# Exchanging the queues of the first loads and reordering the first and last batch of a cross-attention kernel

## The chip, the core and the metric

The kernel runs on one core of one Trainium2 chip. The metric is the device time of one execution in microseconds (us); lower is better. Three timed runs of the kernel before the change gave 660.87, 660.82 and 661.15 us, median 660.87. One more execution was profiled; every view below is of that one.

## The reference

For each of 8 batches, `x1` (512 x 1024) gives queries and `x2` (512 x 1024) gives keys and values; the attention is taken over the 1024 positions and `x1` is added to the result.

```python
q = einsum('bcn,dc->bnd', x1, Wq) + bq                # d = 64
k = einsum('bcn,dc->bdn', x2, Wk) + bk[:, None]
v = einsum('bcn,dc->bdn', x2, Wv) + bv[:, None]       # 512 channels
attn = softmax(einsum('bnd,bdm->bnm', q, k), axis=2)  # 1024 x 1024
out = einsum('bcm,bnm->bcn', v, attn) + x1
```

## The kernel before

All data are float32, and the large products are split: an operand becomes a high part `h`, a low part `l` and a sum part `d` in the format fp32r, and one product is three matmul passes. ScalarE (ACT) rounds the high parts and copies out of PSUM, VectorE (DVE) makes the low and sum parts, GpSimd (POOL) reduces over partitions and issues accumulating DMAs, SyncE (SP) issues plain DMAs. Only the first two value units and output units of batch 0 go in plain float32 (`VF`, `RF`), two slower passes for each product, without a split.

The order of all work is written out by hand, in lists of words, and each word is a call of a method of `Batch`. `FIRST` is for batch 0, `MIDDLE` for batches 1 to 6, `LAST` for batch 7; a word with `+` belongs to the next batch, one with `-` to the previous one. Every engine executes its own instructions in the order of the words; between engines semaphores hold an instruction until its data and its buffer are there. The words that matter here:

- `hx.c`, `hw.c` (called by `begin()`): the loads of quarter `c` of the channels of the first chunk of x2 (128 KB each) and of the value weights (256 KB each). `ldx2.0`, `ldx2.1`: the second chunk (512 KB), and the third and fourth together (1 MB). `lwq`: the weights of q and k, and their bias. `lsd`: the bias of v. `ldx1.0`, `ldx1.1`: x1, in halves.
- `wh.z wl.z wd.z w4.z`: the split of the value weights, on ACT and DVE in turn. `xh.k xl.k xd.k`: the split of chunk k of x2 (256 positions, two value units).
- `K`, `Q`: the projections on TensorE (PE); they use all chunks of x2, or all of x1. `ke`, `qe` take them out of PSUM (ACT), `kc`, `qd` copy them to the other half of the partitions (SP's DMAs), `kr kl`, `qr ql` split them.
- value unit j (128 positions): `VX.j` makes two passes into a bank X, `VY.j` one pass into a bank Y that `sy.j` has filled with the bias (ACT); `cy.j` copies Y out (ACT), `jn.j` joins both (DVE). `vh vl vd` split a pair of units.
- `S.h.i`: scores; `Sc.h.i` copies them out (ACT); `F.Q T.Q L.u E.u` maximum, subtraction and exponential; `es a1 a2 a3 tot few rec r2` the sums; `H.u l.u d.u` split the exponentials of unit u; `R.u.m` is the product with the values; `oy o oa st` take it out, add x1 and store it.

Banks and tiles go round: X and Y have 3 banks each, the scores and projections (`sc`) 2, and x1 and x2 share 2 buffers. `begin()` also runs 10 small matmuls on zeros (`ps_warm`) ahead of the first real one. In the head of the program SP has the four `hx` and ACT the four `hw`:

```python
for c in range(CT):
    states[0].hx(c)      # nc.sync.dma_start(... x2[0, :, 0, c])
    states[0].hw(c)      # nc.scalar.dma_start(... wvT[c])
```

Of the kernel before, what the change touches and what calls it, by code (L numbers as in the profile page):

```python
# [35 lines left out]
vd.2 S.1.5 S.1.3 Sc.1.3 T.0 L.0 E.0 F.1 S.1.6 S.1.4 Sc.1.4 Sc.1.5 L.1 E.1 es.0 VX.6 jn.6 RF.0.0 T.1 L.2 L.3
S.1.7 a1.0 Sc.1.6 RF.0.1 RF.0.2 RF.0.3 RF.0.4 Sc.1.7 F.2 RF.0.5 +ldx2.0 +qd +qr +ql sy.7 VY.7 cy.7 jn.7 vh.3
T.2 L.4 E.2 H.2 a2.0 a3.0 +ldx2.1 +K +ke +kc RF.1.0 L.5 vl.3 vd.3 tot.0 few.0 RF.1.1 RF.1.2 RF.0.6 RF.0.7 l.2
d.2 E.3 H.3 es.1 l.3 a1.1 d.3 E.5 RF.1.3 RF.1.4 E.4 H.4 es.2 rec.0 r2.0 of.0 oa.0 st.0 RF.1.5 RF.1.6 RF.1.7
R.2.0 R.2.1 R.2.2 H.5 R.2.3 F.3 R.2.4 R.2.5 R.2.6 R.2.7 R.3.0 R.3.1 a2.1 a3.1 +kr +kl +S.0.0 +S.0.1 +Sc.0.0  # L40
+Sc.0.1 R.3.2 of.1 R.3.3 l.4 T.3 L.7 E.7 H.7 d.4 +S.0.2 +Sc.0.2 R.3.4 R.3.5 R.3.6 l.5 l.7 +S.0.3 +Sc.0.3 a1.2
a2.2 a3.2 L.6 +S.0.4 +Sc.0.4 R.3.7 +S.0.5 +Sc.0.5 R.4.0 R.4.1 +S.0.6 tot.1 few.1 rec.1 d.5 d.7 oa.1 st.1 tot.2
few.2 +S.0.7 R.4.2 R.4.3 R.4.4 R.4.5 R.4.6 R.4.7 r2.1 oy.2 oy.3 o.2 o.3 oa.2 oa.3 st.3 +Sc.0.6 +Sc.0.7 +F.0
E.6 H.6 es.3 l.6 a1.3 d.6 rec.2 r2.2 oy.4 st.2 +T.0 +L.0 +L.1 +E.0 +E.1 +es.0 +F.1 o.4 oa.4 st.4 a2.3 a3.3
R.5.0 R.5.1 R.5.2 R.5.3 R.5.4 R.5.5 R.5.6 R.5.7 oy.5 o.5 oa.5 st.5 +xh.0 +xl.0 +xh.2 +xl.2 +xd.0 +xh.1 +xl.1
# [37 lines left out]
def kernel(  # L83
# [45 lines left out]
    def bank(tag, name):  # L129
        return psum.tile([P, H], F32, tag=tag, name=name, bufs=BUFS[tag])  # L130

    class Batch:
# [30 lines left out]
        def hx(self, c):  # L163
            if c == 0:
                self.x2[0] = new([P, 2, CT, QN], "x", "x2_0_0")
            nc.sync.dma_start(self.x2[0][:, 0, c, :], x2[0, :, 0, c])

        def hw(self, c):
            if c % 2 == 0:
                wraw[c // 2] = new([P, 2, C], "kd", f"w_raw{c // 2}")  # L170
            nc.scalar.dma_start(wraw[c // 2][:, c % 2, :], wvT[c])

        def lwq(self):
            nc.sync.dma_start(wqk_sb, wqk)
            nc.sync.dma_start(bqk_sb, bqk)
# [339 lines left out]
    def begin():  # L515
        for c in range(CT):
            states[0].hx(c)
            states[0].hw(c)
# [1 line left out]
        nc.vector.memset(spark, 0.0)  # L520

        for i, times in enumerate((4, 3, 3)):
            ps = bank("Y", f"ps_warm{i}")
            for k in range(times):
                nc.tensor.matmul(
                    ps, warm, warm.unsqueeze(1).to_broadcast([P, 4, P]), start=(k == 0), stop=(k == times - 1)
                )
# [48 lines left out]
```

## Time and profile before

| what | value |
|---|---|
| median of 3 timed runs | 660.87 us (660.82 to 661.15) |
| the profiled execution's own time | 661.69 us |
| its span on the core | 659.9 us |
| PE busy | 652.8 us, 99% |
| DVE busy | 619.0 us, 94% |
| ACT busy | 452.4 us, 69% |
| POOL busy | 203.5 us, 31% |
| DMA, mean over the span | 137 GB/s |
| granted TensorE clock, by slices | 9 tenths or more in all 40 |

The own time of the profiled execution is 1.8 us longer than its span: that much lies before the first and behind the last instruction. Engines run side by side, so the shares do not add. PE is busy nearly all the time; a busy PE row does not say that its passes run at their best rate. What can change the time is where PE has nothing to do: at the beginning, at the end and where it waits.

### The profile page before, as it was taken

To read this page: it belongs to the slowest core of one execution; us is meant where nothing else is said; L and a number is where in the kernel's file an instruction comes from. 1 tells how busy PE (TensorE), PEld (TensorE's weight loads), DVE (VectorE), ACT (ScalarE), POOL (GpSimd) and SP (SyncE) were. 2 spreads that over 40 slices of the span, in tenths; PEclk is the share of its full clock that TensorE was granted. 3 is DMA by queue.
4 is the path that set the end of the run, shared out by engine and by line. 5 is a ranking of instruction groups with operands and counts; after the bars stand their busy time and mean duration, and the time that the engine had idled before them with its cause. 6 is when DMAs were issued, how large, how long until landed. Compare 5 with 4: busy or idle time off the path is not lost.

```text
span 659.9 us, 8059 instructions
## 1 busy us (share of the span) xinstructions
PE 652.8 (99%) x2802; PEld 492.4 (75%) x2802; DVE 619.0 (94%) x689; ACT 452.4 (69%) x670; POOL 203.5 (31%) x162
## 2 busy tenths in 40 slices
PE   8999999999999999999999999999999999999997
PEld 3664888677886688866888668886688776887886
DVE  4789999999999999999999999999999999999994
ACT  5688676876587675876767757677675975759542
POOL 0014432323414333043520335212352214412451
PEclk9999999999999999999999999999999999999999
DMA  8534648364665647474563745737367275632374
GB/s 316 191 96 107 119 98 221 73 201 96 129 175 112 175 98 163 124 173 120 114 173 96 216 100 111 173 83 224 81 128 179 77 207 98 126 81 49 93 150 124
DMA packets 41464, 90.21 MB, mean 137 GB/s; under 512 B 13136, under 2 KB 13904, under 8 KB 37712
## 3 DMA queue, kind: packets, MB, share of 16 engines
q0 software_dynamic: 13536, 33.04, 30.0%
q1 hardware_dynamic: 27312, 55.62, 25.4%
q10 hardware_dynamic: 576, 1.05, 0.4%
q8 instruction: 22, 0.36, 0.2%
q14 instruction: 18, 0.15, 0.1%
HBM read 51.91 MB, written 16.78 MB: 104 GB/s over the span
## 4 chain that ended last, share of the span: by engine, by line
PE 96%; DMA 2%; ACT 1%; DVEq 0%; issue 0%; ACTq 0%; DVE 0%
PE ps_oX L426 34%; PE ps_oY L426 17%; PE ps_vX L386 17%; PE ps_s L262 9%; PE ps_vY L386 8%; PE ps_k L205 4%; PE ps_q L205 4%; PE ps_o L451 2%; DMA x<-in_x_dram 1%; DMA w_raw<-in_wvT_dram 1%; ACT eh L297 0%; ACT e L293 0%; ACT ps_vY L382 0%; ACT vy L401 0%; ACT es L312 0%; ACT vh L408 0%
## 5 line engine op out<-in xcount | busy, mean ns | idle before, releaser
L426 PE MATMUL ps_oY<-vd,ed 128*128 128x512 f32 x496 | 193.2, 392 | 0.0
L426 PE MATMUL ps_oX<-vh,eh 128*128 128x512 f32 x496 | 193.0, 389 | 0.0
L426 PE MATMUL ps_oX<-vl,el 128*128 128x512 f32 x496 | 193.0, 389 | 0.0
L426 PEld LDWEIGHTS ps_oY<-vd,ed 128*128 128x128 f32 x496 | 93.1, 188 | 25.0 <-issue 5.1
L506 POOL DMA_DIRECT2D o<-in_x1T_dram x62 | 55.6, 916 | 171.6 <-ACT o L503 97.6
L426 PEld LDWEIGHTS ps_oX<-vl,el 128*128 128x128 f32 x496 | 93.1, 188 | 19.5
L426 PEld LDWEIGHTS ps_oX<-vh,eh 128*128 128x128 f32 x496 | 93.1, 188 | 19.3 <-issue 0.2
L293 ACT ACTIVATE e<-e 128x1024 f32<-128x1024 f32 x64 | 67.9, 1062 | 49.6 <-DVE e L290 48.3
L267 ACT COPY e<-ps_s 128x512 f32<-128x512 f32 x128 | 70.9, 589 | 28.6 <-PE ps_s L262 27.6
L329 POOL PARTITION_ALL_REDUCE den<-es x32 | 80.7, 2522 | 26.0 <-DVE es L319 25.0
L306 DVE SCALAR_TENSOR_TENSOR ed<-el,eh 128x1024 fp32r<-128x1024 f32 x62 | 83.0, 1341 | 2.1
L315 POOL DMA_DIRECT2D es<-e x32 | 28.6, 895 | 179.1 <-ACT es L312 166.9
L301 DVE TENSOR_TENSOR el<-e,eh 128x1024 fp32r<-128x1024 f32 x62 | 79.5, 1298 | 0.0
L290 DVE TENSOR_TENSOR e<-e,top 128x1024 f32<-128x1024 f32 x64 | 77.0, 1231 | 0.0
L282 POOL PARTITION_ALL_REDUCE top<-max x32 | 46.9, 1466 | 68.0 <-DVE max L278 67.9
L386 PE MATMUL ps_vX<-wh,xh 128*128 128x512 f32 x248 | 67.6, 394 | 0.0
L386 PE MATMUL ps_vY<-wd,xd 128*128 128x512 f32 x248 | 65.9, 393 | 0.8 <-ACT ps_vY L382 0.8
L386 PE MATMUL ps_vX<-wl,xl 128*128 128x512 f32 x248 | 66.3, 389 | 0.0
L297 ACT ACTIVATE eh<-e 128x1024 fp32r<-128x1024 f32 x62 | 64.6, 1054 | 0.5
L401 ACT COPY vy<-ps_vY 128x512 f32<-128x512 f32 x62 | 36.4, 591 | 40.0 <-PE ps_vY L386 38.8
L386 PEld LDWEIGHTS ps_vX<-wh,xh 128*128 128x128 f32 x248 | 45.8, 188 | 15.7 <-DVE max L277 4.1
L386 PEld LDWEIGHTS ps_vY<-wd,xd 128*128 128x128 f32 x248 | 46.2, 188 | 12.5 <-ACT ps_vY L382 1.6
(59 smaller groups left out, 963.5 us busy)
## 6 DMA issues: line engine op xcount, KB each, us to landing
x<-in_x_dram SPq DMA_DIRECT2D x29, 1024.0 KB, 6.6
es<-e POOLq DMA_DIRECT2D x32, 512.0 KB, 4.6
out_dram<-o SPq DMA_DIRECT2D x63, 256.0 KB, 2.4
o<-in_x1T_dram POOLq DMA_DIRECT2D x62, 256.0 KB, 4.3
x<-in_x_dram SPq DMA_DIRECT2D x5, 512.0 KB, 10.3
k<-k SPq DMA_DIRECT2D x16, 128.0 KB, 2.2
q<-q SPq DMA_DIRECT2D x16, 128.0 KB, 2.4
w_raw<-in_wvT_dram ACTq DMA_DIRECT2D x4, 256.0 KB, 4.1
```

The costliest lines, as they stand in the source:

```text
L205: nc.tensor.matmul(ps[r, :], wqk_sb[:, which, c, :], x(h, c), start=(c == 0), stop=(c == CT - 1))
L262: nc.tensor.matmul(ps, k[:, ts(i, P)], self.qa[:, ts(h, H)], start=(z == 0), stop=(z == 1))
L267: nc.scalar.copy(self.half[h][:, :, i, :], self.ps[h, i].rearrange("p (q n) -> p q n", q=2))
L290: nc.vector.tensor_tensor(e, e, top, ALU.subtract)
L293: nc.scalar.activation(self.unit(u), self.unit(u), AF.Exp)
L297: nc.scalar.activation(self.e[u]["h"], self.unit(u), AF.Copy, scale=SPLIT)
L301: nc.vector.tensor_tensor(self.e[u]["l"], self.unit(u), f32(self.e[u]["h"]), ALU.subtract)
L306: nc.vector.scalar_tensor_tensor(e["d"], f32(e["l"]), -T, f32(e["h"]), ALU.mult, ALU.add)
L329: nc.gpsimd.partition_all_reduce(self.den[Q], self.es[Q][:, 0, :], P, ReduceOp.add)
L386: nc.tensor.matmul(ps, self.c[j // 2][z][:, c, ts(j % 2, P)], w[z][:, c, :], start=(start and c == 0), stop=(stop and c == CT - 1), skip_g ...
L426: nc.tensor.matmul(ps, self.e[u][z][:, m, :], self.v[m // 2][z][:, m % 2, :], start=start, stop=stop, skip_group_check=True,)
L506: nc.gpsimd.dma_start(self.o[u], x1T[self.b, ts(u, P), :], accum_op=ALU.add)
```

## The change

The same 336 words of `FIRST` and 235 words of `LAST` stand in another order; no word is added or removed, and `MIDDLE` is untouched. In the head, `hx` goes to ACT's queue and `hw` to SP's, the load of the bias of q and k moves from SP (`lwq`) to the end of ACT's head loads, and one of the ten warming matmuls is left out. On PE the float32 passes of units 0 and 1 now go quarter by quarter (`VF.0.c VF.1.c`), and behind `K` come `VY.3`, `VX.2`, `Q`, `VX.3`, `VY.2`, `VY.4`, `VX.5`, `VY.5`, `VX.4` and then the first scores. The methods `xh`, `xl`, `xd` can leave out half of a chunk (`apart`), but with `WHOLE = 2` the test `k == 0.5` is never true, and they do what they did.

In a few words the change was described as: head's loads exchanged between the queues, first passes of value unit 2 ahead of k's projection, order of first and last batch anew with delays in mind. In the list itself `K` stands ahead of `VX.2`, as before.

```diff
-VF.0.0 VF.1.0 VF.1.1 wh.0 VF.1.2 VF.1.3 wl.0 wd.0 w4.0 wh.1 wl.1 wd.1 w4.1 VF.0.1 VF.0.2 VF.0.3 lwq ldx2.0
-ldx2.1 xh.1 lsd K xl.1 xh.2 xh.3 ldx1.0 bv ke xd.1 xl.2 xl.3 VX.2 ldx1.1 jf.0 xd.2 xd.3 sy.2 sy.3 sy.5 jf.1 Q
-kc VY.2 VY.3 qe kr cy.2 cy.3 vh.0 qd kl jn.2 vl.0 qr sy.4 VX.3 jn.3 vh.1 VX.4 VY.5 cy.5 vd.0 VX.5 VY.4 cy.4 ql
-S.0.0 S.0.1 S.0.2 S.0.3 S.0.5 Sc.0.0 Sc.0.1 Sc.0.2 Sc.0.3 S.0.4 Sc.0.4 Sc.0.5 S.0.6 Sc.0.6 S.0.7 Sc.0.7 S.1.1
...
+wh.0 VF.0.0 VF.1.0 wl.0 VF.0.1 VF.1.1 wd.0 wh.1 VF.0.2 VF.1.2 wl.1 VF.0.3 VF.1.3 wd.1 w4.1 ldx2.0 lwq xh.1
+xl.1 xd.1 w4.0 ldx2.1 lsd K xh.3 bv xl.3 jf.0 xd.3 sy.2 sy.3 sy.4 jf.1 VY.3 cy.3 ldx1.0 ke VX.2 xh.2 xl.2 xd.2
+vh.0 vl.0 vd.0 ldx1.1 Q kc qe kr VX.3 kl VY.2 cy.2 jn.2 jn.3 sy.5 +ldx1.0 qd qr VY.4 cy.4 VX.5 vh.1 VY.5 cy.5
+VX.4 ql S.0.0 S.0.1 S.0.2 S.0.3 S.0.7 Sc.0.0 Sc.0.1 Sc.0.2 Sc.0.3 S.0.4 Sc.0.4 jn.4 jn.5 vh.2 vl.1 vd.1 vl.2
...
 LAST = """
...
-vh.0 vl.0 d.1 E.3 es.1 sy.3 VY.3 H.0 l.0 cy.2 jn.2 sy.4 VY.4 cy.3 jn.3 d.0 a3.0 Sc.1.2 a1.1 vd.0 sy.5 vh.1
-vl.1 a2.1 S.1.4 vd.1 S.1.3 Sc.1.3 Sc.1.4 tot.0 few.0 cy.4 jn.4 -r2.3 -os.6 -oa.6 -st.6 VY.5 cy.5 VX.5 jn.5
+vh.0 vl.0 d.1 E.3 es.1 sy.3 VY.3 H.0 l.0 cy.2 jn.2 sy.4 VY.4 cy.3 jn.3 a3.0 Sc.1.2 a1.1 vd.0 sy.5 vh.1 vl.1
+a2.1 vd.1 S.1.3 Sc.1.3 tot.0 few.0 cy.4 jn.4 S.1.4 Sc.1.4 d.0 -r2.3 -os.6 -oa.6 -st.6 VY.5 cy.5 VX.5 jn.5 VX.6
...
-... H.3 r2.0 T.2 L.4 L.5 E.4 E.5 es.2 d.2 R.2.0 ... lt a1.2 H.5 d.3 ...
+... H.3 r2.0 T.2 L.5 L.4 E.5 H.5 E.4 es.2 d.2 R.2.0 ... lt a1.2 d.3 ...
-... rec.3 r2.3 oy.6 oy.7 t.6 t.7 o.6 o.7 st.6 st.7 p.7 sq.7
+... rec.3 r2.3 oy.6 oy.7 t.6 o.6 st.6 t.7 o.7 st.7 p.7 sq.7
...
+    WHOLE = 2
...
         def hx(self, c):
...
-            nc.sync.dma_start(self.x2[0][:, 0, c, :], x2[0, :, 0, c])
+            nc.scalar.dma_start(self.x2[0][:, 0, c, :], x2[0, :, 0, c])
         def hw(self, c):
...
-            nc.scalar.dma_start(wraw[c // 2][:, c % 2, :], wvT[c])
+            nc.sync.dma_start(wraw[c // 2][:, c % 2, :], wvT[c])
         def lwq(self):
             nc.sync.dma_start(wqk_sb, wqk)
-            nc.sync.dma_start(bqk_sb, bqk)
...
+        def apart(self, k):
+            return slice(P, QN) if self.first and k == WHOLE / 2 - 0.5 else slice(0, QN)
...
             states[0].hw(c)
+        nc.scalar.dma_start(bqk_sb, bqk)
...
-        for i, times in enumerate((4, 3, 3)):
+        for i, times in enumerate((3, 3, 3)):
```

More of the change, by code (lines that the diff above doesn't have):

```diff
@@ L36 @@
[L36 to L45, printed above, removed]
@@ new lines @@
+VX.4 ql S.0.0 S.0.1 S.0.2 S.0.3 S.0.7 Sc.0.0 Sc.0.1 Sc.0.2 Sc.0.3 S.0.4 Sc.0.4 jn.4 jn.5 vh.2 vl.1 vd.1 vl.2
+S.0.6 S.0.5 Sc.0.5 Sc.0.6 Sc.0.7 F.0 T.0 L.0 L.1 F.1 S.1.1 sy.6 +ldx1.1 +Q +qe S.1.0 Sc.1.0 Sc.1.1 S.1.7 vd.2
+VX.6 S.1.2 Sc.1.2 E.0 VY.6 cy.6 jn.6 S.1.4 T.1 L.2 L.3 S.1.3 Sc.1.3 Sc.1.4 VX.7 S.1.6 +ldx2.0 E.1 es.0 S.1.5
+Sc.1.5 Sc.1.6 Sc.1.7 F.2 RF.0.0 RF.0.1 RF.0.2 RF.0.3 RF.0.4 a1.0 +qd +qr +ql RF.0.5 E.2 H.2 l.2 E.3 H.3 es.1
+a2.0 a3.0 +ldx2.1 +K +ke +kc RF.1.0 RF.1.1 RF.1.2 sy.7 VY.7 cy.7 RF.1.3 RF.1.4 RF.1.5 T.2 L.4 L.5 E.4 H.4 +kr
@@ new lines @@
+jn.7 vh.3 RF.0.6 RF.1.6 RF.0.7 a1.1 d.2 F.3 tot.0 few.0 rec.0 r2.0 of.0 oa.0 st.0 a2.1 E.5 H.5 es.2 l.3 a3.1
+RF.1.7 R.2.0 R.2.1 R.2.2 R.2.3 R.2.4 R.2.5 of.1 +kl +S.0.0 +S.0.1 +Sc.0.0 +Sc.0.1 d.3 R.3.0 R.3.1 R.3.2 +S.0.2
++Sc.0.2 R.3.3 +S.0.3 +Sc.0.3 +S.0.4 +Sc.0.4 R.3.4 R.3.5 vl.3 T.3 L.6 L.7 E.7 +S.0.5 +Sc.0.5 H.7 vd.3 R.2.6
+R.3.6 R.2.7 R.3.7 l.4 d.4 R.4.0 a1.2 a2.2 +S.0.6 +Sc.0.6 l.5 R.4.1 tot.1 few.1 rec.1 r2.1 oy.3 a3.2 d.5 +S.0.7
+l.7 d.7 oa.1 st.1 oy.2 o.2 tot.2 few.2 R.4.2 R.4.3 R.4.4 R.4.5 R.4.6 R.4.7 oa.2 st.2 o.3 oa.3 st.3 +Sc.0.7
@@ L48 @@
++F.0 E.6 H.6 es.3 l.6 a1.3 d.6 +xh.0 rec.2 r2.2 oy.4 +T.0 +L.0 +L.1 +E.0 +E.1 +es.0 +xh.1 o.4 oa.4 st.4 +xl.0
++xd.0 +F.1 R.5.0 R.5.1 R.5.2 R.5.3 R.5.4 R.5.5 R.5.6 R.5.7 oy.5 o.5 oa.5 st.5 a2.3 +xl.1 a3.3 +xd.1 +xh.3
++xl.3 R.6.0 R.6.1 R.6.2 R.6.3 R.6.4 R.6.5 R.6.6 R.6.7 oy.6 o.6 R.7.0 R.7.1 R.7.2 R.7.3 +sy.0 R.7.4 R.7.5 R.7.6
+R.7.7 oy.7 o.7 +xh.2 +xl.2 +xd.2 +sy.1 +S.1.0 +Sc.1.0 +S.1.1 +Sc.1.1 tot.3 few.3 rec.3
 """
@@ L348, in chunk @@
             return self.x2[k // 2][:, k % 2]
+        def apart(self, k):
+            return slice(P, QN) if self.first and k == WHOLE / 2 - 0.5 else slice(0, QN)
         def xh(self, k):
+            at = self.apart(k)
             self.c[k] = {"h": new([P, CT, QN], "kh", f"xh_{self.b}_{k}", FR)}
-            nc.scalar.activation(self.c[k]["h"], self.chunk(k), AF.Copy, scale=-SPLIT)
+            nc.scalar.activation(self.c[k]["h"][:, :, at], self.chunk(k)[:, :, at], AF.Copy, scale=-SPLIT)
         def xl(self, k):
-            self.c[k]["l"] = new([P, CT, QN], "kl", f"xl_{self.b}_{k}", FR)
-            nc.vector.tensor_tensor(self.c[k]["l"], self.chunk(k), f32(self.c[k]["h"]), ALU.add)
+            c, at = self.c[k], self.apart(k)
+            c["l"] = new([P, CT, QN], "kl", f"xl_{self.b}_{k}", FR)
+            nc.vector.tensor_tensor(c["l"][:, :, at], self.chunk(k)[:, :, at], f32(c["h"][:, :, at]), ALU.add)
         def xd(self, k):
-            c = self.c[k]
+            c, at = self.c[k], self.apart(k)
             c["d"] = new([P, CT, QN], "kd", f"xd_{self.b}_{k}", FR)
-            nc.vector.scalar_tensor_tensor(c["d"], f32(c["l"]), T, f32(c["h"]), ALU.mult, ALU.add)
+            nc.vector.scalar_tensor_tensor(
+                c["d"][:, :, at], f32(c["l"][:, :, at]), T, f32(c["h"][:, :, at]), ALU.mult, ALU.add
+            )
         def VF(self, j, c):
```

15 lines of the change are left out of this document (6 added, 9 removed).

## The prediction

> **What bounds the kernel now.** I read the page's busy shares first, then PE's waits, then the chain of waits, then the head's timeline.
>
> ```profile
> PE 652.8 (99%) x2802; PEld 492.4 (75%) x2802; DVE 619.0 (94%) x689; ACT 452.4 (69%) x670; POOL 203.5 (31%) x162
> PE ps_k L205 <- DMA x<-in_x_dram: 1.4, 1, 1.4
> PE ps_warm L525 <- DVE spark L520: 1.0, 1, 1.0
> PE ps_vY L386 <- ACT ps_vY L382: 0.8, 1, 0.8
> PE ps_s L262 <- ACT e L267: 0.2, 1, 0.2
> 14.51 3.65 PE ps_k L205 x14
> 18.16 2.04 PE ps_vX L386 x8
> 20.20 3.58 PE ps_q L205 x16
> ...
> 590.30 0.92 PE ps_vY L386 x4
> 591.25 0.59 ACT vy L401
> ```
>
> PE has four waits in the whole execution. One is the start, one is in the head (K waits for a load), and two are in the last batch. In the chain PE stands alone from 14.51 to 591: each piece begins where the one before it ended. A new order of the same words can therefore gain nothing in that stretch; it can only bring new waits. What can be gained lies ahead of 14.51, in the 1.0 us of waits in batch 7, and behind the last matmul.
>
> **The head, as it is.**
>
> ```profile
> 0.73 4.17 ACTq L171 DMA_DIRECT2D w_raw<-in_wvT_dram  x4
> 0.73 1.80 SPq L166 DMA_DIRECT2D x<-in_x_dram  x4
> 2.58 0.43 SPq L174 DMA_DIRECT2D wqk_sb<-in_wqk_dram  x1
> 4.32 0.33 SPq L175 DMA_DIRECT2D bqk_sb<-in_bqk_dram  x1
> 4.56 0.34 ACTq L171 DMA_DIRECT2D w_raw<-in_wvT_dram  x1
> 5.12 0.80 SPq L161 DMA_DIRECT2D x<-in_x_dram  x2
> 8.39 0.30 PEld L366 LDWEIGHTS ps_v<-w_raw,x 128*128 128x128 f32 x2 [0.77 <-DMA w_raw<-in_wvT_dram]
> 12.02 0.19 PEld L205 LDWEIGHTS ps_k<-x,wqk_sb 128*64 128x64 f32 x2 [0.76 <-DMA x<-in_x_dram]
> 14.51 0.20 PEld L205 LDWEIGHTS ps_k<-x,wqk_sb 128*64 128x64 f32 x4 [2.30 <-DMA x<-in_x_dram]
> GB/s 0 0 42 190 300 356 382 391 395 354 284 360 257 333 410 391 404 431 399 429 421 421 421 197 87 33 49 208 98 0 0 0 0 0 167 199 191 279 355 448
> ```
>
> Eight loads are issued by 3 us; the ninth and tenth (bias, fourth weight quarter) go out only at 4.32 and 4.56, as the first ones land. So the fourth quarter of wv comes late, and PE's float32 passes stop for about 0.5 us until 8.39. Then K begins at 12.02, when the second chunk of x2 is there, and stops until 14.51 for chunks 3 and 4 (`ldx2.1`, 1 MB). The last row is the bandwidth in slices of 0.75 us from 0 to 30: it is at 380 to 430 GB/s except for a ramp (42, 190, 300) and a weak stretch from 6.75 to 10.5 (354, 284, 360, 257, 333).
>
> **The change, part by part.**
>
> *Exchange of the queues, bias to ACT, quarters in step.* SP now has the four weight loads, so the fourth goes out near 2.1 instead of 4.56, and `VF.0.3 VF.1.3` come last. 16 passes at 0.43 (successive rows 8.92 and 9.35 of the same line below) are 6.9 us; from a start near 4.6 they end near 11.5 instead of 11.9. The 0.5 us stop goes. What is late next is K: its second pair of matmuls still needs chunks 3 and 4, and K stands ahead of every other PE work that is ready. So the stop moves into the wait for `ldx2.1`, and only the landing of that load counts, one for one. The wait of the ninth and tenth load stays: it now falls on the bias (ACT) and chunk 2 (SP, near 4.5 instead of 5.12). Behind the bias on ACT wait the table load and `wh.0`, as they did behind the fourth weight load until 4.9; their result is first used behind K. Behind chunk 2 on SP wait wqk and `ldx2.1`.
>
> When does `ldx2.1` land? Ahead of it in the same bandwidth lie, before and after, the same bytes: 4 x 128 KB, 4 x 256 KB, 256 KB for wqk, 512 KB and its own 1 MB. Only lost bandwidth can be won. Best end: the weak stretch fills up to 395: (41 + 111 + 35 + 138 + 62) x 0.75 us = 290 KB, at 390 GB/s 0.74 us, and the queue that starts first carries rows of double size in the first slice (42 x 0.75 = 32 KB, 0.1 us): 0.85 us earlier. Worst end: `ldx2.1` has to wait one 256 KB load longer for its turn, 0.66 us later. Before, that stretch was not short of issued loads (5.12 and 5.6 lie well ahead of it), and reissuing them sooner gives it nothing; the row it is nearest to is the same load's own landing at 14.5. I take 0.2 us earlier: the ramp's 0.1 and a small part of the weak stretch. [...]
>
> *One warming matmul less.*
>
> ```profile
> 3.94 0.15 PEld L525 LDWEIGHTS <-warm 128*128 128x128 bf16 x1 [0.28 <-issue]
> 4.37 0.14 PEld L525 LDWEIGHTS <-warm 128*128 128x128 bf16 x1 [0.28 <-issue]
> 4.63 0.41 PEld L366 LDWEIGHTS ps_v<-w_raw,x 128*128 128x128 f32 x2
> 8.92 0.19 PEld L366 LDWEIGHTS ps_v<-w_raw,x 128*128 128x128 f32 x1 [0.24 <-issue]
> 9.35 0.19 PEld L366 LDWEIGHTS ps_v<-w_raw,x 128*128 128x128 f32 x1 [0.24 <-issue]
> ```
>
> 0.26 us at most (4.37 to 4.63), and hidden by the wait for `ldx2.1`: nothing. If that cover went, the first passes would still wait for the first weights near 4.5, so 0.1.
>
> *The order behind K.* PE's work from K to the first scores is the same: before VX.2, Q, VY.2, VY.3 and so on, after VY.3, VX.2, Q, then VX.3, VY.2, VY.4, VX.5, VY.5, VX.4. VY.3 needs the bank filled by `sy.3`, behind `xh.3`, `bv` and `sy.2` on ACT: 14.3, 1.06 for a rounding (the row of `qr` below) and three times 0.59 (the copy of 128x512 above) make 17.1, ahead of K's end near 18. `cy.3` now stands ahead of `ke` on ACT and holds it for VY.3's 0.9 us and its own 0.6, with k's copies behind it; k is next used after q, so nobody waits. The tight place is q.
>
> ```profile
> 23.83 1.40 ACT L212 ACTIVATE q<-ps_q,bqk_sb 64x512 f32<-64x512 f32 x2 [2.59 <-PE ps_q L205]
> 29.78 1.06 ACT L235 ACTIVATE qa<-q 128x1024 fp32r<-128x1024 f32 x1 [1.41 <-DMA q<-q]
> 31.39 1.22 DVE L238 TENSOR_TENSOR qa<-q,qa 64x1024 fp32r<-64x1024 f32 x1
> 32.69 0.19 PEld L262 LDWEIGHTS ps_s<-qa,kh 128*128 128x128 f32 x1
> q<-q SPq DMA_DIRECT2D x1, 128.0 KB, 2.2
> q<-q SPq DMA_DIRECT2D x1, 128.0 KB, 4.4
> x<-in_x_dram SPq DMA_DIRECT2D x29, 1024.0 KB, 6.6
> ```
>
> Before, q's second copy was issued when `qe` was done (23.83 + 1.40 = 25.2) and landed 4.4 us later; its rounding began at once (29.78), and the scores began in the moment that `ql` was done (31.39 + 1.22 = 32.61 to 32.69). After: K from 14.3 to 17.95, VY.3 0.92 (the chain's row of four passes), VX.2 twice that, 1.84, and 0.1 for changing over, so Q from 20.8 to 24.4, 0.6 us later than before, and `qe` done at 25.8; the copy, then `qr` and `ql`, 1.06 and 1.22. The scores' turn on PE is at 24.4 + 3 x 1.84 + 3 x 0.92 = 32.7. With a copy of 2.2 us q is ready at 30.3, with 4.4 us at 32.5: only just. Ahead of `qd` on SP now stands batch 1's first x1 load (1 MB), which stood behind it. It needs only k's copies issued ahead of it and the first x2 buffer, free when K ends, and `ke` ends near 21 (17.95 + 0.92 + 0.6 + 1.4), so it has some 4 us of lead, and its bytes (1 MB at 400 GB/s, 2.6 us) are mostly through when the copies come. I put in 0.1 us, between 0 and the 2.0 of the second rival.
>
> *The rest of FIRST.* The same words, with no PE wait before, so 0 at best. In the list, the producers that PE waits for (`Sc` for reused banks, `d` for `R`, `jn` for reused X banks) still stand several words ahead of their users. I take 0, with 0.5 us at the other end (half of batch 7's 1.0, where the order is as tight).
>
> *LAST.*
>
> ```profile
> 601.14 1.22 DVE L306 SCALAR_TENSOR_TENSOR ed<-el,eh 128x1024 fp32r<-128x1024 f32 x1
> 607.53 1.28 DVE L404 SCALAR_TENSOR_TENSOR v<-ps_vX,vy 128x512 f32<-128x512 f32 x2
> 608.26 1.21 PE L386 MATMUL ps_vX<-wh,xh 128*128 128x512 f32 x4
> 618.68 3.25 DVE L290 TENSOR_TENSOR e<-e,top 128x1024 f32<-128x1024 f32 x2
> 621.86 1.21 DVE L306 SCALAR_TENSOR_TENSOR ed<-el,eh 128x1024 fp32r<-128x1024 f32 x1
> 623.13 0.50 PE L426 MATMUL ps_oY<-vd,ed 128*128 128x512 f32 x1
> 656.25 0.48 DVE L491 SCALAR_TENSOR_TENSOR o<-ps_oX,r,oy 128x256 f32<-128x256 f32 x1 [1.55 <-PE ps_oX L426]
> ```
>
> The 0.8 us wait of VY.4 is for `sy.4` on ACT (L382 in the list of waits), and ACT's order up to it is unchanged: it stays. `S.1.4` and `S.1.3` change places, but the third score of the group still needs the copy out of the first: the 0.2 us stays. `d.0` (1.22 at 601.14) moves behind `jn.4`, which comes forward from 607.53 and frees the bank of VX.7 a little sooner (0.68 each for the two joins: 608.2, against VX.7's 608.26). That is given back at 623.13: R.2.0 begins when `d.2` is done (621.86 + 1.21), at the end of DVE's unbroken work, whose sum is the same. `H.5` ahead of `E.4` and `es.2` delays `es.2` by 1.06 us; its next user, `a1.2`, comes much later. At the end `o.6` and its store come sooner, but the last pieces wait for PE's last matmul (656.25). Sum 0, between -0.3 and +0.3.
>
> **The sum.** -0.2 + 0.1 + 0 = -0.1 us. On the profiled execution's own time that is 661.69 to 661.6; the median of the runs lies 0.8 below that execution, so 660.87 becomes 660.8.
>
> **The rivals.**
>
> *The stream ahead of K gets much denser.* If the exchange repairs the ramp too (lost against 390: (348 + 200 + 90 + 34) x 0.75 = 504 KB, 1.3 us) along with the weak stretch (0.74), `ldx2.1` lands up to 2 us earlier; three quarters of it are 1.5 us: 659.4. For it: the wait for K is one for one. Against it: the ramp is the same number of loads from the same two queues. 0.12.
>
> *q's copy is held behind the 1 MB load now ahead of it on SP* (slower). Place: `qr`, then `ql`, then all scores. If the copy takes 6.6 us, as a 1 MB load does, q is ready at 34.7 and S.0.0 begins 2.0 us late: 662.8. It decides from a landing more than 4.6 us after issue. Against it: the load has 4 us of lead. 0.07.
>
> *PE's clock falls back in the longer pause.* The warming rows are 0.43 apart while PE starts and 0.26 at the last: PE began at half its rate. PE would pause from 11.5 to 14.3, broken by one pair of K near 12. Half rate for K adds its 3.6 us once more: 664.4. Against it: after the pause that ends at 14.51 now, K took 3.65, no longer than Q's 3.58 without a pause. 0.03. [...]
>
> *The change does what its description says, not its list:* value unit 2 ahead of K fills 0.9 us of the pause (four passes; the other four need `w4.0`, which stands behind `xh.1` on ACT and ends near 14): 659.9. The list has K first. 0.02.
>
> **How the numbers follow.** The forecast has 0.76: 660.8, by its bounds (-0.85 to +0.66, q up to 0.5, the rest 0.3) 660.0 to 661.9. With half of the first rival, the range is 659.6 to 662.0. A measurement of this kernel tells about 0.2%, 1.3 us, from no change. Faster than 659.5: the first rival and a tail, 0.13. Slower than 662.2: q's copy, the clock and unseen waits in FIRST, 0.10. Within: 0.77.
>
> **What would show it.** Right: K's second pair waits for x until 14.0 to 14.6; no wait in the float32 passes; PE unbroken from K to batch 7; VY.4's 0.8 us wait still there. Wrong: K going on before 13.5, a wait of ps_s for qa near 32.7, K longer than 4 us from its last load, or a wait of PE for DVE between 40 and 120.

## The result, and the profile after

The changed kernel is slower: 663.27 us median of five runs (663.06 to 664.76) beside 660.87 for the kernel before; the ratio is 1.0043 with a 95% interval of [1.0032, 1.0054]. The prediction was 660.8 in a range of 659.6 to 662.0. The profiled execution of the changed kernel took 663.27 us, its span is 661.5.

From the page after: the busy shares, and the chain that ended last by engine.

```profile
PE 654.5 (99%) x2801; PEld 493.0 (75%) x2801; DVE 619.4 (94%) x689; ACT 452.7 (68%) x670; POOL 202.6 (31%) x162
PE 90%; DVE 6%; ACT 1%; issue 1%; DMA 1%; POOL 0%; DVEq 0%; SPq 0%; POOLq 0%
```

PE's waits after, without the one at the start (total, times, longest, in us):

```profile
PE ps_vY L395 <- ACT ps_vY L391: 1.0, 2, 0.8
PE ps_s L263 <- ACT e L268: 0.8, 3, 0.4
PE ps_oY L435 <- DVE ed L307: 0.3, 1, 0.3
PE ps_oY L435 <- DVE r L339: 0.2, 1, 0.2
```

K's wait for its load (1.4 before) is gone from the list, and new waits for ACT and DVE are there. Where they are, the chain after shows (start, length):

```profile
12.79 4.38 PE ps_k L206 x16
...
91.73 2.25 DVE e L291 x2
102.45 2.64 POOL den L330
105.64 4.90 DMA few<-den
111.42 2.27 DVE e L291 x2
...
147.66 3.58 PE ps_k L206 x16
548.95 3.58 PE ps_k L206 x16
```

The chain before was PE alone from 14.51 to 591. Ahead of batch 7, this one leaves PE between 91 and 121 and runs through DVE, a total on POOL (`tot.3`), its small loads (`few.3`) and DVE again. The last two rows are K as it stands in the words of batches 1 and 6 (each makes the k of the next batch). In the chain of the kernel before the same two are:

```profile
146.76 3.58 PE ps_k L205 x16
547.51 3.58 PE ps_k L205 x16
```

Five middle batches, whose words nobody touched, take 401.29 us after and 400.75 before, without a single wait of PE in either: 0.11 us more per batch. Two losses, then: one between 90 and 121, one spread evenly over the batches behind it.

For the runs below I use one number of the trace that the head hardly disturbs: the time from the first pass of R.2.0 (at 66.56 before, 65.58 after) to the end of the span. It is 593.36 us before and 595.92 after, 2.56 more: 1.88 up to the first of these rows, 0.54 between the two, 0.14 behind. It comes from one profiled execution of each kernel; in six kernels that should agree in it (before, new head, new LAST, and below all tiles moved by 64 and `vd.3` by 512 and 1024) it lies between 593.29 and 593.52, so a difference under 0.2 tells nothing. The head itself varies from execution to execution: in the nine profiles of this study with the old head the first value pass behind K begins between 16.33 and 18.64, in the eleven with the new head between 16.37 and 19.91 (medians 17.55 and 16.98). The profile of before in the prediction was a late one (18.09).

Each ratio is against runs of the kernel before on the same chip (medians 660.65 to 660.87).

| kernel | median us | ratio to before [95%] | R.2.0 to end |
|---|---|---|---|
| before | 660.87 | 1 | 593.36 |
| after | 663.27 | 1.0043 [1.0032, 1.0054] | 595.92 |
| new head alone | 660.68 | 0.9997 [0.9988, 1.0006] | 593.29 |
| new LAST alone | 660.97 | 1.0005 [0.9997, 1.0014] | 593.36 |
| before, vd.3 displaced | 661.81 | 1.0017 [1.0009, 1.0026] | 594.03 |
| after, vd.3 as before | 662.7 | 1.0032 [1.0020, 1.0044] | 595.54 |
| new order up to F.2 | 660.98 | 1.0007 [0.9997, 1.0017] | 593.81 |
| new order behind F.2 | 663.24 | 1.0031 [1.0020, 1.0043] | 595.14 |

### The profile page after: what moved, and what is told of

The parts are those of the page before. It is cut to its first block, busy times and chain, and to the rows that moved or that the text cites. A ratio compares the mean times of both kernels' runs of the same rounds, so it can differ in the third digit from the quotient of the medians.

```text
span 661.5 us, 8060 instructions
## 1 busy us (share of the span) xinstructions
PE 654.5 (99%) x2801; PEld 493.0 (75%) x2801; DVE 619.4 (94%) x689; ACT 452.7 (68%) x670; POOL 202.6 (31%) x162
## 4 chain that ended last, share of the span: by engine, by line
PE 90%; DVE 6%; ACT 1%; issue 1%; DMA 1%; POOL 0%; DVEq 0%; SPq 0%; POOLq 0%
PE ps_oX L435 32%; PE ps_oY L435 16%; PE ps_vX L395 14%; PE ps_s L263 8%; PE ps_vY L395 7%; PE ps_k L206 4%; PE ps_q L206 4%; PE ps_o L460 2%; DVE e L291 1%; PE ps_v L375 1%; DVE vl L422 1%; DVE v L413 1%; DMA few<-den 1%; DVE vd L427 1%; PE ps_warm L535 1%
## 5 line engine op out<-in xcount | busy, mean ns | idle before, releaser
L307 DVE SCALAR_TENSOR_TENSOR ed<-el,eh 128x1024 fp32r<-128x1024 f32 x62 | 81.4, 1313 | 2.2
L283 POOL PARTITION_ALL_REDUCE top<-max x32 | 44.8, 1401 | 68.8 <-DVE max L279 68.8
```

Of the source, the lines that this page charges most:

```text
L307: nc.vector.scalar_tensor_tensor(e["d"], f32(e["l"]), -T, f32(e["h"]), ALU.mult, ALU.add)
```

## The experiments

### Which part of the change: head, tail, LAST

The head alone: all of the change up to `S.0.3` (queues, bias load, nine warming matmuls, order), then the old order.

```diff
-FIRST = <before>                       # begin(), hx, hw, lwq as after
+FIRST = <after up to S.0.3> + <the other words in before's order>
 LAST = <before>
```

> The head of the change alone: queues exchanged, bias load moved, nine warming matmuls, and the new order of FIRST up to S.0.3; the rest of FIRST in the order of before, LAST as before. vd.3 then lies at byte 217536, as before. Theory: the head gains what the changed kernel's trace shows at R.2.0, 0.98 us, and nothing of it is given back: 659.9. Rival 'given back': VectorE, whose work is the same, takes the gain away at batch 0's end (R.6.0 waits for d.6, 0.4 us) or the queue exchange costs it elsewhere: 660.5 to 660.9. By the prediction's step the head gives 0.2: 660.7.

Measured: 660.68 us beside 660.65, ratio 0.9997 [0.9988, 1.0006], R.2.0 to the end 593.29. The head gives nothing back later, as the theory said, but the 659.9 that the theory forecast did not come: of the 0.98 us that the head seemed to gain, the medians show nothing. That was the late load in the one profile of before. The interval leaves room for a gain of 0.8 us or a loss of 0.4.

The new LAST alone:

```diff
-LAST = <before>
+LAST = <after>
```

> The kernel before with the new LAST alone. vd.3 stays at 217536. By the changed kernel's trace: the wait at VX.7 (0.14) goes, that at R.2.0 grows from 0.19 to 0.44 and what lies behind it stays: +0.1, 660.9. By the prediction's step: 0, within 0.3. Rival: LAST is where the time was lost: over 661.5.

Measured: 660.97 beside 660.74, 1.0005 [0.9997, 1.0014], and 593.36 from R.2.0 to the end: LAST costs nothing that can be told.

The tail of FIRST alone, on the kernel before:

```diff
-FIRST = <before>
+FIRST = <before up to S.0.3> + <the other words in after's order>   # vd.3 at byte 217536
```

> The kernel before with the new order of FIRST behind S.0.3 alone; head, queues, warming matmuls and LAST as before, and vd.3 at byte 217536, as before. Theory 'sums late': PE's waits at R.6.0 (0.36) and at the scores at the border to batch 1 (1.3) come back although the head is the old one: +1.2 to +1.7, 661.9 to 662.4. Rival 'early PE': the waits are there only because the new head sends PE into the same VectorE work 0.7 to 1 us earlier; with the old head under 0.4 is lost: 660.7 to 661.1.

Measured: 662.6 beside 660.77, 1.0040 [1.0025, 1.0054], 595.22. The old head with the new tail has the loss, so the early PE is not its reason. By the starts of its passes PE stops 0.41 at R.6.0 and 0.47, 0.50 and 0.42 at the border, 1.80 of the 1.86 that this kernel takes longer from R.2.0 to the end. Its profiled execution happened to begin early (first value pass at 16.33), so its trace alone would leave the early PE open; but the changed kernel with `vd.3` as before, whose profiled execution came to R.2.0 only at 68.36, has the four stops too (0.66, 0.47, 0.52 and 0.42).

### What the border between batch 0 and batch 1 does

Timeline of DVE before, then after, around the border (start, length, and in brackets the idle time ahead). L319 and L320 are the folds `a2.3 a3.3`, L491 and L500 `o.5`, L338 and L339 `rec.3`:

```profile
96.81 1.14 DVE L319 TENSOR_TENSOR es<-es 128x512 f32<-128x512 f32 x2
97.87 0.74 DVE L491 SCALAR_TENSOR_TENSOR o<-ps_oX,r,oy 128x512 f32<-128x512 f32 x1
98.53 3.40 DVE L356 TENSOR_TENSOR xl<-x,xh 128x1024 fp32r<-128x1024 f32 x2
...
109.80 0.16 DVE L338 RECIPROCAL r<-few 128x2 f32<-128x2 f32 x1
```

```profile
95.82 1.23 DVE L368 SCALAR_TENSOR_TENSOR xd<-xl,xh 128x1024 fp32r<-128x1024 f32 x1
...
99.47 0.74 DVE L500 SCALAR_TENSOR_TENSOR o<-ps_oX,r,oy 128x512 f32<-128x512 f32 x1
100.14 0.68 DVE L320 TENSOR_TENSOR es<-es 128x512 f32<-128x512 f32 x1
...
101.87 0.42 DVE L320 TENSOR_TENSOR es<-es 128x256 f32<-128x256 f32 x1
...
103.34 2.12 DVE L363 TENSOR_TENSOR xl<-x,xh 128x1024 fp32r<-128x1024 f32 x1
...
110.63 0.17 DVE L339 RECIPROCAL r<-few 128x2 f32<-128x2 f32 x1 [1.58 <-DMA few<-den]
```

And POOL, before and after (`oa.5`, then the total `tot.3`):

```profile
98.91 0.86 POOL L506 DMA_DIRECT2D o<-in_x1T_dram  x1 [0.82 <-DVE o L491]
99.49 2.06 POOL L329 PARTITION_ALL_REDUCE den<-es  x1
```

```profile
100.52 0.87 POOL L515 DMA_DIRECT2D o<-in_x1T_dram  x1 [4.67 <-DVE o L500]
102.45 2.63 POOL L330 PARTITION_ALL_REDUCE den<-es  x1 [1.06 <-DVE es L320]
```

In the new order the split of x2 (`+xl.0 +xd.0`, 2.4 us) stands ahead of the folds and of `o.5`; the total begins at 102.45 where it began at 99.49, and `rec.3`, which DVE must do before anything of batch 1, waits 1.58 us for it. PE pays behind DVE and ACT:

```profile
115.91 0.50 PE L263 MATMUL ps_s<-qa,kh 128*128 128x512 f32 x1 [0.26 <-ACT e L268]
118.84 0.50 PE L263 MATMUL ps_s<-qa,kh 128*128 128x512 f32 x1 [0.36 <-ACT e L268]
119.82 1.20 PE L395 MATMUL ps_vY<-wd,xd 128*128 128x512 f32 x4 [0.25 <-ACT ps_vY L391]
```

By the starts of the passes on either side these three stops cost 0.42, 0.52 and 0.42 us, and R.6.0 another 0.36 behind the pass of 91.22, where PE stands until DVE has done `d.6` (at 91.66; the list puts it down to the small `rec.2` beside it): 1.72 us in four stops. The kernel before has none over 0.11 there.

The folds put back:

```diff
-... o.4 oa.4 st.4 +xl.0 +xd.0 +F.1 R.5.0 ... o.5 oa.5 st.5 a2.3 +xl.1 a3.3 +xd.1
+... o.4 oa.4 st.4 a2.3 a3.3 +xl.0 +xd.0 +F.1 R.5.0 ... o.5 oa.5 st.5 +xl.1 +xd.1
```

> The changed kernel with the words a2.3 a3.3 (the two folds of the last sums of batch 0, VectorE) put back ahead of +xl.0 +xd.0 +F.1. Theory 'sums late': the total tot.3 began at 102.46 (before 99.49) since these folds stood behind that work; its small loads land at 110.54 and VectorE waits 1.58 us for them ahead of batch 1, which is 0.86 us late from there on and PE waits three times for ScalarE's copies of scores. With the folds back VectorE waits at most 0.3 there, PE's offset against the kernel before stays near -0.5 at the border instead of +0.8: about 1.3 us less, 662.0. Rival 'only the head and the places': PE's three waits come from VectorE's and ScalarE's other work; under 0.3 us less, 663.0 to 663.3.

Measured: 663.56, 1.0037 [1.0023, 1.0051], 595.66. DVE's wait fell to 0.13, yet the expected gain did not come. The total still began at 102.55, since `oa.5` on POOL stands ahead of it; and with DVE no earlier PE now stops for the bank that `o.6` frees:

```profile
107.74 1.19 PE L395 MATMUL ps_vX<-wh,xh 128*128 128x512 f32 x4 [0.74 <-DVE o L500]
```

Folds and split both put back, vd.3 in its old place:

```diff
-... st.4 +xl.0 +xd.0 +F.1 R.5.0 ... o.5 oa.5 st.5 a2.3 +xl.1 a3.3 +xd.1
+... st.4 a2.3 a3.3 +F.1 R.5.0 ... o.5 oa.5 st.5 +xl.0 +xd.0 +xl.1 +xd.1
```

> The changed kernel with vd.3 at byte 217536 (as in the kernel before) and with +xl.0 +xd.0 of VectorE put back behind o.5, the folds a2.3 a3.3 put back ahead of +F.1. Moving the folds alone left the total tot.3 where it was (102.55), because POOL's queue holds oa.5 ahead of it and oa.5 waits for o.5, which ended at 101.6 behind +xl.0 +xd.0 (2.4 us); in the kernel before o.5 ended at 98.6. Theory 'two splits ahead of o.5': tot.3 begins near 100, its loads land near 108, VectorE's wait of 1.58 falls under 0.3 and PE's waits at the border to batch 1 fall from 1.3 to under 0.3: 662.6 less 1.2, 661.4 (left: 0.35 at R.6.0 and what LAST costs). Rival 'work of VectorE as such': PE is as far behind at batch 1's Q as in the changed kernel, only with other waits (as when the folds were moved: 0.9 at VX.2): 662.4 to 662.7.

Measured: 662.2, 1.0024 [1.0014, 1.0034], 595.05, where the kernel with vd.3 alone put back has 595.54. The stops at the scores are gone, but one of 1.19 stands at VX.2, again for `o.6`, and R.6.0 still stops 0.41. The rival was nearer: DVE is behind whatever stands last at the border.

So it is late before the border. From R.2.0 on DVE works with next to no pause (busy 22.89 us of the 23.31 before, 24.21 of the 24.56 after), and `d.6` begins 23.31 us after R.2.0 in the kernel before, 24.56 in the changed one. The first row is of before, the second of after:

```profile
89.87 1.52 DVE L306 SCALAR_TENSOR_TENSOR ed<-el,eh 128x1024 fp32r<-128x1024 f32 x1
90.14 1.52 DVE L307 SCALAR_TENSOR_TENSOR ed<-el,eh 128x1024 fp32r<-128x1024 f32 x1
```

My next guess was the 1.20 us that DVE idles for POOL's maximum behind F.0:

```diff
-... F.0 T.0 L.0 L.1 F.1 ... S.1.7 vd.2 VX.6 ...
+... F.0 T.0 vd.2 L.0 L.1 F.1 ... S.1.7 VX.6 ...      # vd.3 as before
```

> The changed kernel with vd.3 at byte 217536 and one word moved: vd.2 (VectorE, 1.2 us) goes between T.0 and L.0. In the changed order F.0 T.0 L.0 stand in a row, so VectorE waits 1.20 us for POOL's maximum (T.0) with nothing to do; in the kernel before vl.2 vd.2 stood there and VectorE did not wait. From 52 us on VectorE has next to no idle time in both kernels, so what it loses here reaches d.6 (R.6.0 waits 0.35 for it), o.6 and the border to batch 1. Theory 'VectorE's idle time ahead of 52': VectorE is about 1.2 earlier at d.6, the wait of R.6.0 goes and the waits at the border shrink: from R.2.0 to the end 594.3 to 594.6 (595.5 without the move, 593.3 in the kernel before), median 661.4 to 661.7. Rival 'border only': what counts is the wait of 1.58 for few.3 at the border, which is made by the words there; 595.4, median 662.6.

Measured: 663.15, 1.0037 [1.0023, 1.0050], 596.32: no gain, and the guess fell; PE's first stop at the scores even grew from 0.42 to 1.53. The timelines of POOL and DVE say why. After (maximum on POOL, then DVE's subtraction), and then with `vd.2` in the gap:

```profile
40.43 1.06 POOL L283 PARTITION_ALL_REDUCE top<-max  x1 [40.00 <-DVE max L279]
46.50 1.96 POOL L283 PARTITION_ALL_REDUCE top<-max  x1 [5.00 <-DVE max L279]
41.53 2.36 DVE L291 TENSOR_TENSOR e<-e,top 128x1024 f32<-128x1024 f32 x2 [1.20 <-POOL top L283]
48.49 2.36 DVE L291 TENSOR_TENSOR e<-e,top 128x1024 f32<-128x1024 f32 x2 [0.35 <-POOL top L283]
```

```profile
39.72 1.96 POOL L283 PARTITION_ALL_REDUCE top<-max  x1 [39.28 <-DVE max L279]
46.68 1.06 POOL L283 PARTITION_ALL_REDUCE top<-max  x1 [5.00 <-DMA q<-q]
41.71 2.36 DVE L291 TENSOR_TENSOR e<-e,top 128x1024 f32<-128x1024 f32 x2 [0.96 <-POOL top L283]
47.78 2.36 DVE L291 TENSOR_TENSOR e<-e,top 128x1024 f32<-128x1024 f32 x2 [0.59 <-POOL top L283]
```

In these rows POOL's maximum takes 1.06 us where DVE is idle, or about to be, and 1.96 where DVE has just begun a work of 1.22. Filling the first gap made that maximum 0.90 longer and emptied the second: 1.55 us of idle time in both kernels.

All four repairs at once:

```diff
-FIRST = <after>, LAST = <after>
+FIRST = <after with vd.2, the folds and the split moved as above>, LAST = <before>   # vd.3 as before
```

> The changed kernel with all four repairs: vd.3 at byte 217536, vd.2 between T.0 and L.0, +xl.0 +xd.0 behind o.5 and a2.3 a3.3 ahead of +F.1, and LAST as before. If the places, VectorE's 1.2 us idle behind F.0, the two splits ahead of o.5 and LAST are the whole loss, from R.2.0 to the end it takes 593.3 to 593.8 and the median is 660.5 to 660.9, no slower than the kernel before. If VectorE loses time elsewhere in the new order too, PE keeps a wait at VX.2 for o.6: 594.2 to 594.8, 661.4 to 661.9.

Measured: 662.44, 1.0021 [1.0010, 1.0033], 594.64. Still 1.28 more than before from R.2.0 to the end; PE stops 1.00 at VX.2 and 0.22 at R.6.0. So the new order loses in more places than those, and I split it in two at `F.2`. Up to F.2 new, the rest old (vd.3 and LAST as before):

```diff
-FIRST = <after>
+FIRST = <after up to F.2> + <the other words in before's order>
```

> The changed kernel with vd.3 at byte 217536 and LAST as before, and FIRST cut in two behind F.2: up to F.2 the new order, from there to the end the order of before. Theory 'early part': VectorE loses its time ahead of 52 us (4.6 us idle behind 25 us against 2.2 in the kernel before, POOL's maxima among them), so that d.6 is 1.2 later against R.2.0 here too; PE waits at R.6.0 or VX.2: from R.2.0 to the end 594.2 to 594.6, median 661.2 to 661.8. Rival 'late part': the order behind F.2 costs it (sums, splits ahead of o.5, collisions with POOL's totals): 593.3 to 593.6, median 660.5 to 660.8.

And the other way round, new head, old order up to F.2, then new:

```diff
-FIRST = <after>
+FIRST = <after up to S.0.3> + <before's words up to F.2> + <the others in after's order>
```

> The counterpart: up to F.2 the new head and then the order of before, from there the new order; vd.3 at byte 217536, LAST as before. Theory 'early part': VectorE arrives early, PE waits only at the border for what few.3 makes late: from R.2.0 to the end 593.6 to 594.2, median 660.8 to 661.4. Rival 'late part': it carries the whole loss of 2: 595.0 to 595.4, median 662.2 to 662.6.

Measured: the early part 660.98, 1.0007 [0.9997, 1.0017], 593.81; the late part 663.24, 1.0031 [1.0020, 1.0043], 595.14. My theory was the wrong one of the two. From R.2.0 to the end the early part, with all of DVE's waits for the maxima in it, costs 0.45, which the medians cannot tell from nothing; the late part costs 1.78. It has the four stops of the changed kernel (0.40, 0.35, 0.51, 0.41), the early part has none over 0.18. Its `d.6` begins 24.56 behind R.2.0 as in the changed kernel (23.76 with the early part), and `rec.3` waits as it does there. The first row is of the early part, the second of the late one:

```profile
108.93 0.15 DVE L340 RECIPROCAL r<-few 128x2 f32<-128x2 f32 x1
110.98 0.17 DVE L340 RECIPROCAL r<-few 128x2 f32<-128x2 f32 x1 [1.50 <-DMA few<-den]
```

### The loss without a wait: where vd.3 lies

Tiles get their places in the on-chip memory in the order in which the words first ask for them. Before, `vd.3` asks ahead of `den`, `few` and `r` and lies at byte 217536 of a partition; in the new order it asks last, behind these (1152 bytes) and the `o` tiles, at 224832. All other tiles of PE's fp32r passes, streams and weights, begin 448 bytes behind a multiple of 2048, `vd.3` now 1600. In the changed kernel's trace just the 122 passes that stream `vd.3` begin 0.234 us ahead of the next pass; the usual distance of the others is 0.227.

> The changed kernel with one edit: the tile vd of the last value pair (vd.3) and the three o tiles exchange their places in the on-chip memory, so that vd.3 begins at byte 218688 of a partition and no longer at 224832, its end. The order of all work stays. Theory 'place': in the changed kernel's trace the 122 passes that stream vd.3 start 0.234 us before the next one, all others 0.227; they will take 0.227 here, and the kernel loses 122 x 0.0075 = 0.9 us: 662.4 instead of 663.27. Rival 'order': all that was lost is lost in waits at the border of batch 0 and batch 1, and the long passes are those of the work beside them, not of the place: 663.2, passes still 0.234.

The edit takes a place for `vd.3` ahead of the first `o` tile:

```diff
         def fresh(self, u):
+            if self.first and not self.o:
+                new([P, 2, C], "vd3", "vd3_place")
```

Measured: 663.5, 1.0043 [1.0030, 1.0057], five middle batches 401.29 as in the changed kernel: no effect. That it lay behind all other tiles is not it; 218688 is 1600 behind a multiple of 2048 as well.

The kernel before with `vd.3` at 224832, and the changed one with it at 217536:

```diff
         def vd(self, p):                          # in before
+            if self.first and p == 3:  <new() of den, few, r, o>
         def tot(self, Q):                         # in after
+            if self.first and Q == 0:
+                new([P, 2, C], "vd3", "vd_place")
```

> The kernel before with one edit: places for den, few, r and o are taken ahead of vd.3, so that vd.3 lies at byte 224832 as in the changed kernel (before: 217536). The order of all work stays as before. Theory 'place': 122 passes at 0.234 instead of 0.227, +0.9 us: 661.8. Rival 'order': no pass becomes longer, 660.9.

> The changed kernel with the place of vd.3 taken ahead of those of den, few and r, so that it lies at byte 217536, as in the kernel before. The order of all work stays. The first try of this kind moved it to 218688 and its passes stayed at 0.234. Theory 'grid': all other tiles that TensorE reads begin 448 bytes behind a multiple of 2048; behind den, few and r (1152 bytes together) a tile begins 1600 behind one, and that makes its 122 passes 0.0075 us longer; at 217536 they take 0.227 and the time is 0.9 us less than the changed kernel's, 662.4 to 662.6. Rival 'order': the passes follow the work beside them, 0.234 here too, 663.3 to 663.5.

K of batches 1 and 6 in the chain, of the kernel before with `vd.3` displaced:

```profile
147.39 3.58 PE ps_k L205 x16
548.69 3.58 PE ps_k L205 x16
```

and of the changed kernel with `vd.3` put back:

```profile
150.77 3.58 PE ps_k L206 x16
551.52 3.58 PE ps_k L206 x16
```

401.30 and 400.75: the place alone moves the middle batches from one value to the other, with the order of work the same in each pair. The times: 661.81 beside 660.65, 1.0017 [1.0009, 1.0026], about the expected 0.9. In the second case they are 662.7 beside the changed kernel's 663.27; their ratios to before, 1.0032 [1.0020, 1.0044] and 1.0043 [1.0032, 1.0054], do not tell the two apart.

Then five kernels on what makes a place good or bad. Gaps of 64 bytes (the last of 32) ahead of seven tiles, with weights at 448, and the same with `den`, `few` and `r` placed ahead, which moves all these tiles, but not the value weights, by 1152:

```diff
         def vh(self, p):                          # likewise vl, vd
+            if self.first and p in (0, 1):
+                gap()                             # 64 unused bytes; for vd also p = 2
```

> The kernel before with unused gaps of 64 bytes ahead of seven tiles, so that the tiles that PE streams begin 448 (vh.2, vl.2, vh.3, vl.3), 512 (vh.0), 576 (vl.0, qa), 640 (vh.1), 704 (vd.0), 768 (vl.1), 832 (vd.1) and 864 (vd.2, vd.3) bytes behind a multiple of 2048, while the tiles that PE loads as weights stay at 448. Nothing else is changed. It measures what one pass takes by the place of its stream. Theory 'grid': some of these places make passes of 0.234 us; if the place counts modulo 1024 or 512, vl.0 and qa at 576 are like 1600: 0.234. If only the distance of 1152 from the weights counts, none here is long: all 0.227.

> As the kernel with gaps, but den, few and r (1152 bytes) take their places ahead of all tiles, so that the weights of the product with the values begin at 1600 behind a multiple of 2048, and the streams at 1600 (vh.2, vl.2, vh.3, vl.3), 1664, 1728, 1792, 1856, 1920, 1984 and 2016. The order of work is that of the kernel before. If the place of the stream by itself counts, vh.2 to vl.3 at 1600 take 0.234 and the time rises by over 1.5 us; if its distance from the weights counts, they take 0.227.

```profile
148.45 3.58 PE ps_k L210 x16
556.35 3.58 PE ps_k L210 x16
```

Measured, one run each (the rows are of the first): 671.91 and 673.72 us, 11.1 and 13.0 more than the 660.77 beside them, five middle batches 407.90 and 409.47. PE's waits are those of the kernel before; its passes mostly take 0.226 to 0.237 instead of 0.227, also some of the passes whose own stream and weights were not moved. Both theories fell: it is no property of one stream's place, nor of its distance from its weights.

All tiles moved by 64 together; `vd.3` displaced by 1024 (`den` ahead of it); by 512 (unused bytes, `few` and `r` ahead of it). The edit shown is the first:

```diff
+    shift = const.tile([P, 16], F32, name="shift")        # ahead of all
```

> The kernel before with 64 unused bytes ahead of all tiles, so that every stream and every weight tile of TensorE begins at 512 behind a multiple of 2048, no longer at 448. The distances between the tiles stay. If only these distances count: 0.227 a pass, 660.7. [...]

> The kernel before with den taken ahead of vd.3, so that vd.3 begins 1472 behind a multiple of 2048, 1024 away from the grid of all other tiles that TensorE reads. Its 122 passes show by which step the place counts: 0.227 if it counts modulo 1024 or less, 0.234 if modulo 2048.

> The kernel before with 512 bytes taken ahead of vd.3 (960 behind a multiple of 2048). 0.227 a pass of vd.3 if the place counts modulo 512 or less, 0.23 or more if modulo 1024 or 2048.

Measured: 660.89, 1.0001 [0.9992, 1.0010], then one run each of 660.42 and 660.72; five middle batches 400.77, 400.73 and 400.74, all passes 0.227. So a common shift is harmless, and so are steps of 512 and 1024; a displacement by 1152, and gaps of 64, cost. That fits a grid of 512 bytes, or of 256, that all tiles share (1152 is 128 more than a multiple of either). No run tried 128 or 256. What in the chip makes it so stays open, and also why with one tile off the grid only its own passes grow, while with the gaps passes on unmoved tiles grow too.

### One try at more

```diff
 LAST = """
-... es.1 sy.3 VY.3 H.0 l.0 cy.2 jn.2 sy.4 VY.4 ...
+... es.1 sy.3 sy.4 VY.3 H.0 l.0 cy.2 jn.2 VY.4 ...      # FIRST as in the head alone
```

> The head of the change with the rest of FIRST and LAST as before (660.68 when it was run), and one more edit: in LAST the word sy.4 (ScalarE writes the bias into the bank of unit 4) moves directly behind sy.3, ahead of H.0 and cy.2, which both the kernel before and the changed one have in front of it. PE's wait of 0.93 at VY.4 goes; H.0 and cy.2 come 0.6 later, behind which nothing of PE is due before 605. Theory: 0.9 less, 659.8. Rival: the wait comes back at R.0.0, whose parts l.0 and d.0 VectorE makes later: 660.4 to 660.8.

Measured: 660.98, 1.0008 [0.9999, 1.0017], 593.88. VY.4's wait fell from 0.8 to 0.3 and came back elsewhere: 0.7 at a VX pass for DVE, 0.7 at the scores (0.2 before). No kernel here is clearly faster than the kernel before.

## Why the prediction was wrong, by its own steps

**The rest of FIRST, "I take 0, with 0.5 us at the other end",** is the step that failed. Measured from R.2.0 to the end, 0.45 up to F.2 and 1.78 behind it. Its reason was that the producers PE waits for stand several words ahead of their users. That looks at PE's neighbours in the list only. What matters is how late the producing engine is when it comes to those words, and DVE works with next to no pause there, in both kernels. In that stretch the order of DVE's words is a schedule of its own: `+xl.0 +xd.0` ahead of `o.5` and the folds made POOL's total 2.96 us later, and that came back to DVE itself as a wait of 1.58. That chain is a part of the loss only: with the folds alone put back the wait was gone, and PE stopped elsewhere instead. The step of the prediction that had the right idea stands two paragraphs further on, for LAST: there it asked what DVE has to do in sum and when it ends.

How much of the 1.78 each word carries is not settled. Putting the border back gave 0.49 (595.54 to 595.05); that step, LAST and the filled gap together gave 0.90 (594.64). The rest is in DVE's being 1.25 us late at `d.6`, and the traces show where most of that comes from: works of DVE that meet POOL. Between R.2.0 and `d.6` three of them in each kernel run beside a maximum or a total on POOL. Beyond their usual length (the median of the same operation in the trace of before) they take 2.01 us before, 2.84 after, 2.85 with the late part and 2.01 with the early one. The longest is `a3.1`, a fold that usually takes 0.42, beside the maximum `T.3`:

```profile
66.85 1.48 DVE L320 TENSOR_TENSOR es<-es 128x256 f32<-128x256 f32 x1
67.15 1.36 POOL L283 PARTITION_ALL_REDUCE top<-max  x1
```

That is 0.83 of the 1.25; the remainder is which words stand in that stretch. No run moved these works, so what it would give back is not shown. From `d.6` to `rec.3` it is the other way round (2.23 us before, 1.15 after), so such works do not explain the loss at the border.

**What was not in the prediction at all:** that the order of the words decides the places of tiles, and that the place of one tile lengthens passes. It is 0.54 us over five middle batches, and 0.38 to 0.67 from R.2.0 to the end. With the others, 0.45 + 1.78 + 0.00 (LAST) + 0.38 = 2.61, beside 2.56 measured. That they meet so closely is in part luck: with 0.67 the sum is 2.90, and the early and the late part need not add.

**The head: -0.2, between -0.85 and +0.66.** Right as far as the runs tell: 0.9997 [0.9988, 1.0006]. The profile alone would have said 1.0: K goes on in one piece, and the value passes begin at 17.1 where they began at 18.1. That was the late load of the one execution of before: over the profiles the 1 MB load landed between 12.71 and 15.02 with the old head, between 12.57 and 14.59 with the new. Two readings under the term were wrong. The fourth quarter of wv went out at 4.31 and not near 2.1, since the bias went ahead of it as the eighth load, and the ninth goes out only then (before, at 4.32); and K's second pair began at 13.52, ahead of the 14.0 to 14.6 that were to show the step right. The medians agree with no gain at all as well as with 0.2.

**One warming matmul less: nothing.** Right in the time. In the profile after, the first float32 passes begin 0.85 us apart (4.79, 5.65, 6.50), and 0.43 apart only from 7.05 on. That cannot be laid to the missing matmul: with all tiles moved by 64 and ten warming matmuls, 5.22 and 6.07 are 0.85 apart too, and in the late part, with nine, no two are more than 0.54 apart. K's last load, landed at 13.48, hides it.

**q's copy, +0.1; LAST, 0 within 0.3; VY.4's wait stays.** All right: no wait of the scores for q; 1.0005 [0.9997, 1.0014] for LAST; 0.8 in the list of waits. R.2.0 of batch 7, which I put at "the same", waits 0.44 where it waited 0.19.

**The range.** The upper end, 661.9, does not follow from its terms: 0.66 + 0.5 + 0.3 added to 660.87 make 662.3, and FIRST's own 0.5 is not among them. With it the sum is 662.8, still short of 663.27.

**The rivals:** the denser stream and q behind the 1 MB load did not come true. Nor did the falling clock in the result, but a lower clock is real: in the profiled execution of the changed kernel with `vd.3` as before (665.67 us, where the median is 662.7) the granted clock is 0.50 from 14.8 to 18.2, behind the pause in K (0.997 in the mean), and K takes 5.34 us from its last load instead of 3.65. Four more executions, two of them with the old head, have that mean granted clock too and are 3.0 to 3.3 above their medians. So these executions lose less than the 3.6 forecast, and the lower clock does not set the two heads apart. The slower end that did come in the result was named only as "unseen waits in FIRST" inside the 0.10, without a mechanism or a price, though the signs listed at the end ("a wait of PE for DVE between 40 and 120") named it exactly.

## What to carry to other kernels

Where PE is the bound but another engine is busy without a pause, read that engine's own timeline before calling a reordering free: ask what each of its words releases, and whether the answer comes back to it. A change of order that touches first uses also changes the places of tiles; look for passes that grew without a wait, and compare a stretch of unchanged code (here K to K) before looking for waits. Take the spread of the head from several executions before reading a gain out of one profile.

## What the runs showed of the hardware

The place of tiles: 64-byte gaps between PE's tiles cost 11.1 us of 660 (671.91 beside 660.77), and a tile 1152 bytes off the others' grid 0.007 us on each pass that streams it (0.234 against 0.227). With the gaps PE's passes took mostly 0.226 to 0.237 us, by nothing but the places of tiles. No run shows whether PE waits for anything there.

DVE and POOL: a maximum on POOL took 1.06 us beside an idle DVE, 1.96 where DVE had just begun a work of 1.22, and 1.36 beside `a3.1`, which itself took 1.48 instead of 0.42; a work of DVE that takes 1.22 took 2.12 beside a total on POOL. In the kernel with the filled gap `vd.2` ran from 39.53 to 40.75, and the maximum that began at 39.72 took 0.90 longer, near the 1.03 that `vd.2` still had to run. The work beside the total began at 103.34, with 1.74 us of the total still to run, and grew by 0.90, about half of that. What holds one of the two up is not shown.
